# Three 512-column adds through a PSUM tile in place of two adds in SBUF, in a deformable-convolution kernel

## The chip, the cores and the metric

The kernel runs on one core of a Trainium2 chip. Five engines run side by side, each through its own queue in program order: TensorE (PE, with weight loads shown as PEld), VectorE (DVE), ScalarE (ACT), GpSimd (POOL) and SyncE (SP, which here only issues DMAs). The metric is device time in microseconds of one launch; a smaller one is better. Three runs of the kernel before gave 7886.47, 7887.33 and 7905.6 us, median 7887.33 us.

## The reference: what is computed

The input is x, 2 images of 128 channels and 64 x 64 pixels, f32. Two "metaformer" layers follow each other, each with a token mixer and a feed-forward part, both with normalization ahead and a residual sum. The change lies in the mixer of layer 0: four branches of deformable convolution with kernels of 1, 1, 3 and 7 pixels, 60 taps in all. For each pixel and tap, a predicted offset gives a position between pixels; the input is sampled there bilinearly, scaled by a predicted mask, and multiplied with the tap's weights:

```python
return v00 * (1 - wy) * (1 - wx) + v01 * (1 - wy) * wx + v10 * wy * (1 - wx) + v11 * wy * wx
...
sampled = bilinear_sample(x, py, px) * mask[:, None]
return jnp.einsum('bckhw,ock->bohw', sampled, reg_w.reshape(O, C, k * k))
```

The other parts are: group norm, ReLU and a 1 x 1 "fuse" convolution behind the branches; a mixture of 8 experts (layer 0, feed-forward); a convolution and a state-space scan (layer 1, mixer); and 64 experts that pick their tokens (layer 1, feed-forward).

## The kernel before, in words

**Tiling.** An image is 4096 pixels, 32 tiles of 128. Four tiles (512 pixels) are a group (`GT = 4`), so that an image has 8 groups (`NG`). `L0Conv.run` calls `sample(b, g, ...)` for the 8 groups of image 0 and then for those of image 1. A call goes through the 60 taps, so there are 2 x 8 x 60 = 960 taps in all.

**A tap.** A table in DRAM holds, for each pixel position, the 128 channels of its four neighbours (the corners) side by side, 512 numbers. `gather` (L705) has POOL issue four indirect DMAs, one for each tile: 128 rows of the table, chosen by the index list `idx`, go into `v`, a tile of 128 partitions x 4 tiles x 512 numbers in SBUF. Six buffers of `v` exist (pool `l0v`), and a buffer is taken again once PE has transposed what it held. Then:

- L746: DVE multiplies all 2048 columns of `v` with the four corner weights, which it reads from `pw`, a PSUM tile that L738 fills once for 30 taps. The weight is repeated over the 128 channels.
- L748 and L749: DVE adds the corners, first two and two (1024 columns), then the two sums (512 columns), all in `v`.
- L111: PE transposes the four 128 x 128 sums into the PSUM tile `pst`; L753: ACT copies it to `st`.
- L773 (`product`, two taps later): PE multiplies `st` with the tap's weights `regw` and accumulates the branch in two PSUM tiles `out`. At a branch's end, ACT copies them out (L787).

**The order of the work around it.** Everything is written out by hand, in one program order for each engine. The gather of tap t+1 is written ahead of the multiply of tap t; POOL has nothing else to do meanwhile and runs ahead as far as free buffers of `v` let it. After each tap `conv.step()` adds a piece of the offset convolution of a later group (matmuls on PE at L402, sums at L499 and small arithmetic at L545 to L581 on DVE, which make the indices and the corner weights), and `rest.step()`, called `pace` times, adds a piece of other work: during image 0 the normalization of image 1 and constants, during image 1 what follows image 0's sampling (`after`: the fuse convolution, the layer-0 experts with DVE work at L985 and L1001, and the layer-1 convolutions, whose matmuls are L1146, L1154 and L1173). So this other work is paced by taps. The state-space scan and the last feed-forward part come after the sampling of image 1.

**PSUM.** During the sampling, `p_w` has one bank, `p_t` two, `p_o` two, and the offset convolution or the other work two.

Of the kernel before, what the change touches and what calls it, by code (L numbers as in the profile page):

```python
# [10 lines left out]
F32 = mybir.dt.float32  # L11
I32 = mybir.dt.int32
AF = mybir.ActivationFunctionType
ALU = mybir.AluOpType
AX = mybir.AxisListType
PSUM = bass.MemoryType.PSUM
# [3 lines left out]
P = 128  # L20
B = 2
C = 128
# [3 lines left out]
GT = 4  # L26
# [138 lines left out]
def mixed(gens, n):  # L165

    todo, live = deque(gens), deque()
    while todo or live:
        if todo and len(live) < n:
            live.append(todo.popleft())  # L170
        gen = live.popleft()
        try:
            weight = next(gen)
            live.append(gen)
            yield weight
        except StopIteration:
            pass


def together(gens, n):  # L180
    for _ in mixed(gens, n):
        pass


class L0Conv:
# [416 lines left out]
    def run(self, build, after):  # L602

        env, tc, nc = self.env, self.env.tc, self.env.nc
        pools = lambda ctx: lambda name, bufs, **kw: ctx.enter_context(tc.tile_pool(name=name, bufs=bufs, **kw))
        with ExitStack() as ctx:
            pool = pools(ctx)
            self.rp, self.regw = pool("l0rw", 1), {}
            self.ip = pool("l0i", 2)
            self.vp = pool("l0v", 6)  # L610
            self.stp = pool("l0s", 2)
            self.pending, self.held = [], deque()
            first = ctx.enter_context(ExitStack())
            self.open_offsets(pools(first))
            for i in range(2):
                nc.vector.memset(self.padc[i], 0.0)
            psum = ctx.enter_context(ExitStack())
            right = lambda name: pools(psum)(name, 1, space=PSUM, side="right")
            self.p_f = deque([right("l0po")])
            cur = self.new_group(self.ip)  # L620
            with (
                tc.tile_pool(name="nrm", bufs=3) as sp,
                tc.tile_pool(name="nrmp", bufs=4, space=PSUM) as pp,
            ):
                xs = []
                for g in range(NG):
                    if g % GT == 0:
                        x = self.vp.tile([P, GT, 4 * C], F32, name="v")
                    xs.append(x[:, g % GT, :])
                    nc.sync.dma_start(out=xs[g], in_=env.d["x"][0, :, g * 512 : (g + 1) * 512])  # L630
                xn = self.vp.tile([P, GT, 4 * C], F32, name="v")
                self.load_weights()
                for _ in self.zero_table(0):
                    pass
                own = lambda g: xn[:, g % GT, :].rearrange("p (j c) -> p j c", c=C)
                norms = [self.norm_group(0, g, sp, pp, "nrm", x, own(g)) for g, x in enumerate(xs)]
                together(norms[:2], 2)

                stage = self.rows(0, 0)
                self.sum_weights()  # L640
                others = Side()
                others.add(mixed(norms[2:], 3))
                for _ in range(24):
                    others.step()
                offsets = self.offset_stream([(0, 0, cur)], stage)
                while others.todo:
                    next(offsets)
                    for _ in range(3):
                        others.step()
                self.load_chunk(0)  # L650
                for _ in self.norm_end(0):
                    pass
                for _ in offsets:
                    pass
            self.p_w = pool("l0pw", 1, space=PSUM)
            self.p_t = pool("l0pt", 2, space=PSUM)
            self.p_o = pool("l0py", 2, space=PSUM)
            self.pending = [(n, functools.partial(self.load_chunk, c)) for n, c in ((1, 1), (3, 2))]
            early = psum.enter_context(ExitStack())
            p_m = pools(early)("l0pm", 1, space=PSUM, side="right")  # L660

            def more():

                early.close()
                self.p_f.append(right("l0po2"))
                yield


            conv, rest = Side(), Side()
            self.late, self.made = deque(), [0, 0]  # L670
            rest.add(self.norm(1, p_m, "misc"), more(), build)
            ahead = {}

            def runs():
                for g in range(1, NG):
                    ahead[g] = self.new_group(self.ip)
                    yield 0, g, ahead[g]
                    yield 1, g - 1, None
                yield 1, NG - 1, None

            conv.add(self.offset_stream(runs()))
            for g in range(NG):
                self.sample(0, g, *cur, conv, rest, 2 if g else 3, lambda: ahead.get(g + 1))
                cur = ahead.get(g + 1)
            conv.drain()
            rest.drain()
            psum.close()
            first.close()
            side = ctx.enter_context(tc.tile_pool(name="l0ps", bufs=2, space=PSUM))
            rest.add(after(0, side))  # L690
            cur = self.load_group(1, 0)
            for g in range(NG):
                nxt = self.load_group(1, g + 1) if g + 1 < NG else None
                self.sample(1, g, *cur, conv, rest, 2, lambda: nxt)
                cur = nxt
            for f in self.late:
                f()
            for _, f in self.pending:
                f()
            self.pending = []  # L700
            rest.drain()
# [10 lines left out]
    def sample(self, b, g, idx, w4, conv, rest, pace, after):  # L712

        env, nc = self.env, self.env.nc
        pw, vs = None, {}
        new = lambda: self.vp.tile([P, GT, 4 * C], F32, name="v")

        def fetch(idx, t):
            if t in vs:
                v = vs.pop(t)  # L720
                self.gather(b, v, idx, t, range(2, GT))
            else:
                v = new()
                self.gather(b, v, idx, t, range(GT))
            return v

        if b == 0 and g == 0:
            for i in range(6):
                vs[i] = new()
                self.gather(b, vs[i], idx, i, range(0, 2))  # L730
        if not self.held:
            self.held.append(fetch(idx, 0))
        for br, (k, _) in enumerate(BRANCH):
            for t in range(FIRST[br], FIRST[br] + k * k):
                tw = t % HT
                if tw == 0:
                    pw = self.p_w.tile([P, GT, HT, 4], F32, name="pw")
                    nc.vector.tensor_copy(pw, w4[:, :, t : t + HT, :])  # L738
                if t + 1 < NTAP:
                    self.held.append(fetch(idx, t + 1))  # L740
                elif after():
                    self.held.append(fetch(after()[0], 0))
                v = self.held.popleft()
                v4 = v.rearrange("p j (q c) -> p j q c", q=4)
                w = pw[:, :, tw, :].unsqueeze(3).to_broadcast([P, GT, 4, C])
                nc.vector.tensor_tensor(v4, v4, w, ALU.mult)  # L746
                up = v4[:, :, 0:2, :]
                nc.vector.tensor_tensor(up, up, v4[:, :, 2:4, :], ALU.add)  # L748
                nc.vector.tensor_tensor(v4[:, :, 0, :], v4[:, :, 0, :], v4[:, :, 1, :], ALU.add)  # L749
                pt = self.p_t.tile([P, GT, P], F32, name="pst")  # L750
                transpose4(nc, env.ident, pt, [v4[:, j, 0, :] for j in range(GT)])
                st = self.stp.tile([P, 512], F32, name="st", bufs=3)
                nc.scalar.copy(st, pt.rearrange("p j t -> p (j t)"))  # L753
                self.late.append(functools.partial(self.product, b, g, br, t, st))
                if len(self.late) > 2:
                    self.late.popleft()()
                due = [f for n, f in self.pending if n == 0]
                self.pending = [(n - 1, f) for n, f in self.pending if n]
                for f in due:
                    f()  # L760
                conv.step()
                for _ in range(pace):
                    rest.step()
# [1135 lines left out]
```

## Time and profile before

| | us |
|---|---|
| median of the runs | 7887.33 |
| profiled execution, own time | 7901.31 |
| its span | 7898.7 |
| first and last gather start (L705) | 106.8 and 5734.0 |
| DVE busy | 6077.1 |
| PE busy | 5390.6 |
| POOL busy | 5031.9 |
| mean granted TensorE clock | 0.806 of full speed |

How to read it: all times are from one profiled execution. Some 5630 of the 7900 us are the sampling of the two images, the part in which L705, L746, L748 and L749 run. The 40-slice rows of the page show a busy DVE and POOL and DMA engines between 6 and 8 tenths busy there:

```profile
DVE  5878878888887887788898667787756665789992
...
POOL 4777777777777777777777666676743334357640
PEclk8888788888788878878878778877886788877789
DMA  7887767777676778877777777777754344434444
```

In a group's row, "idle before" is the time in which the engine did nothing just ahead of these instructions, and the arrow names what ended most of it. DVE instructions that follow each other without a wait overlap by some 0.08 us in the records.

### The profile page before, as it was taken

What the parts mean: (1) busy time and instruction counts of PE and PEld (TensorE: products, weight loads), DVE (VectorE), ACT (ScalarE), POOL (GpSimd) and SP (SyncE); (2) the same over time, 40 slices, a digit from 0 to 9 for tenths busy, and PEclk for the clock granted to TensorE, in tenths of its full rate; (3) what the DMA queues carried; (4) which work ended last, traced back from release to release, by engine and by line L of the source; (5) the groups of instructions that cost most, each with busy time, mean ns of one, the idle gap of its engine ahead of it and who ended that gap; (6) DMA issues with size and microseconds to landing.
All of it is one profiled execution on the core that took longest, in us unless ns stands there. A gap on an engine that the chain in (4) does not pass through costs nothing. (4 is left out here: it accounts for less than half of the span.)

```text
span 7898.7 us, 67414 instructions
## 1 busy us (share of the span) xinstructions
PE 5390.6 (68%) x21313; PEld 3209.2 (41%) x21313; DVE 6077.1 (77%) x6780; ACT 1992.0 (25%) x3838; POOL 5031.9 (64%) x4589
## 2 busy tenths in 40 slices
PE   4667777667776757656666878865565679756668
PEld 3344444444444424324334555532233456412124
DVE  5878878888887887788898667787756665789992
ACT  1211111111111113211111222211163255455540
POOL 4777777777777777777777666676743334357640
PEclk8888788888788878878878778877886788877789
DMA  7887767777676778877777777777754344434444
GB/s 223 261 267 214 224 207 223 214 219 219 210 221 208 224 228 270 265 255 234 240 237 217 217 218 218 228 224 222 206 172 141 107 114 113 114 131 146 146 137 149
DMA packets 645198, 1596.67 MB, mean 202 GB/s; under 512 B 168020, under 2 KB 253180, under 8 KB 640876
## 3 DMA queue, kind: packets, MB, share of 16 engines
q0 software_dynamic: 307200, 1006.88, 42.5%
q1 hardware_dynamic: 306156, 537.52, 21.4%
q10 hardware_dynamic: 31488, 47.97, 1.7%
q8 instruction: 171, 2.80, 0.1%
q14 instruction: 183, 1.50, 0.1%
HBM read 1478.65 MB, written 115.83 MB: 202 GB/s over the span
## 5 line engine op out<-in xcount | busy, mean ns | idle before, releaser
L705 POOL DMA_INDIRECT v<-table,idx x3840 | 4070.0, 1060 | 1628.2 <-issue 1033.8
L746 DVE TENSOR_TENSOR v<-v,pw 128x2048 f32<-128x2048 f32 x960 | 2192.0, 2283 | 665.7 <-DMA v<-table,idx 466.9
L773 PE MATMUL out<-st,regw 128*128 128x512 f32 x3840 | 2270.7, 719 | 187.6 <-issue 118.6
L753 ACT COPY st<-pst 128x512 f32<-128x512 f32 x960 | 557.7, 585 | 4227.9 <-remote 1887.3
L111 PE MATMUL pst<-ident,v 128*128 128x128 f32 x3840 | 730.7, 318 | 1133.6 <-issue 962.4
L748 DVE TENSOR_TENSOR v<-v 128x1024 f32<-128x1024 f32 x960 | 1177.2, 1226 | 34.6 <-remote 1.6
L1420 POOL TENSOR_TENSOR db<-du,bcb 128x512 f32<-128x512 f32 x512 | 656.8, 1288 | 845.3 <-DVE da L1471 698.8
L773 PEld LDWEIGHTS out<-st,regw 128*128 128x128 f32 x3840 | 807.2, 233 | 864.6 <-issue 779.9
L111 PEld LDWEIGHTS pst<-ident,v 128*128 128x128 f32 x3840 | 522.4, 164 | 1512.3 <-issue 1284.6
L1443 PE MATMUL py<-sc,ident 128*128 128x512 f32 x1024 | 660.7, 752 | 230.7 <-DVE sc L1481 230.3
L1471 DVE TENSOR_TENSOR_SCAN da<-da,state,db 128x512 f32<-128x512 f32 x512 | 657.1, 1283 | 183.2 <-ACT da L1427 137.6
L749 DVE TENSOR_TENSOR v<-v 128x512 f32<-128x512 f32 x960 | 664.4, 692 | 33.0
L402 PE MATMUL po<-wa,win 128*128 128x147 f32 x2112 | 381.7, 303 | 118.1 <-issue 110.8
L402 PEld LDWEIGHTS po<-wa,win 128*128 128x128 f32 x2112 | 334.3, 201 | 228.7 <-issue 228.6
L1443 PEld LDWEIGHTS py<-sc,ident 128*128 128x128 f32 x1024 | 200.4, 229 | 529.9 <-DVE sc L1481 438.0
L1146 PEld LDWEIGHTS ps<-ipw,hs 128*120 128x120 f32 x2816 | 356.0, 207 | 121.7 <-ACT X L1108 56.4
L1146 PE MATMUL ps<-ipw,hs 128*120 128x64 f32 x2816 | 355.1, 290 | 55.2 <-ACT X L1108 40.5
L1481 DVE TENSOR_TENSOR sc<-da,bcb 128x512 f32<-128x512 f32 x512 | 354.2, 692 | 43.0 <-PE py L1443 0.5
L1427 ACT ACTIVATE da<-delta,w_A_log 128x512 f32<-128x512 f32 x512 | 354.0, 692 | 18.7 <-DVE delta L1383 2.8
L1154 PE MATMUL ps<-tm,X 120*88 120x48 f32 x2048 | 216.1, 280 | 52.1 <-ACT Y L1108 35.5
L1154 PEld LDWEIGHTS ps<-tm,X 120*88 120x88 f32 x2048 | 211.0, 187 | 98.7 <-ACT Y L1108 47.4
L402 PEld LDWEIGHTS po<-wb,win 128*128 128x128 f32 x960 | 164.2, 210 | 117.2 <-issue 117.1
(296 smaller groups left out, 4704.3 us busy)
## 6 DMA issues: line engine op xcount, KB each, us to landing
bcb<-bc SPq DMA_DIRECT2D x256, 512.0 KB
regw<-in_regw SPq DMA_DIRECT2D x192, 640.0 KB
v<-table,idx POOLq DMA_INDIRECT x3840
yd<-ys ACTq DMA_DIRECT2D x128, 256.0 KB
yc<-yd SPq DMA_DIRECT2D x32, 1024.0 KB
gb<-gd SPq DMA_DIRECT2D x16, 2048.0 KB
wt<-in_weight SPq DMA_DIRECT2D x32, 1024.0 KB
tm<-pos SPq DMA_DIRECT2D x16, 1440.0 KB
```

Source lines behind the costliest of these rows:

```text
L111: nc.tensor.transpose(ps[:, j, :], s, ident)
L402: m()
L705: self.env.nc.gpsimd.indirect_dma_start(out=v[:, j, :], out_offset=None, in_=self.table[b], in_offset=bass.IndirectOffsetOnAxis(ap=idx[:, ...
L746: nc.vector.tensor_tensor(v4, v4, w, ALU.mult)
L748: nc.vector.tensor_tensor(up, up, v4[:, :, 2:4, :], ALU.add)
L749: nc.vector.tensor_tensor(v4[:, :, 0, :], v4[:, :, 0, :], v4[:, :, 1, :], ALU.add)
L753: nc.scalar.copy(st, pt.rearrange("p j t -> p (j t)"))
L773: nc.tensor.matmul(self.out[half], self.regw[t // CH][:, t % CH, half * P : (half + 1) * P], st, start=first, stop=last,)
L1146: nc.tensor.matmul(ps[:, k, :], patch, own, start=True, stop=True)
L1420: nc.gpsimd.tensor_tensor(dbs[u], pieces[k]["du"][:, half, :], bcb[u // 2][:, 0, :], ALU.mult)
L1443: nc.tensor.matmul(py[k, half], by, what, start=first, stop=last)
L1471: nc.vector.tensor_tensor_scan(s, s, dbs.pop(u), state[:, half, n : n + 1], ALU.mult, ALU.add)
```

## The change

A tap's three DVE operations become four. The multiply is the same operation on the same columns. Then corners 0 and 1 are added into `low`, a tile of 512 columns in PSUM; corner 2 is added to `low` in place; and `low` plus corner 3 goes to the place in `v` from which PE transposes. The order of the sum changes from (0+2)+(1+3) to ((0+1)+2)+3. `low` comes from a new PSUM pool `p_r` with one buffer. The gathers, the transposes and all instructions of the other engines stay, in the same order. In the changed kernel the multiply is L747, the adds are L749, L750 and L751, and other lines after them move down by two.

```diff
@@ -653,6 +653,7 @@
             self.p_w = pool("l0pw", 1, space=PSUM)
+            self.p_r = pool("l0pr", 1, space=PSUM)
             self.p_t = pool("l0pt", 2, space=PSUM)
@@ -742,11 +743,12 @@
                 v4 = v.rearrange("p j (q c) -> p j q c", q=4)
-                w = pw[:, :, tw, :].unsqueeze(3).to_broadcast([P, GT, 4, C])
-                nc.vector.tensor_tensor(v4, v4, w, ALU.mult)
-                up = v4[:, :, 0:2, :]
-                nc.vector.tensor_tensor(up, up, v4[:, :, 2:4, :], ALU.add)
-                nc.vector.tensor_tensor(v4[:, :, 0, :], v4[:, :, 0, :], v4[:, :, 1, :], ALU.add)
+                w = pw[:, :, tw, 0:4].unsqueeze(3).to_broadcast([P, GT, 4, C])
+                nc.vector.tensor_tensor(v4[:, :, 0:4, :], v4[:, :, 0:4, :], w, ALU.mult)
+                low = self.p_r.tile([P, GT, C], F32, name="low")
+                nc.vector.tensor_tensor(low, v4[:, :, 0, :], v4[:, :, 1, :], ALU.add)
+                nc.vector.tensor_tensor(low, low, v4[:, :, 2, :], ALU.add)
+                nc.vector.tensor_tensor(v4[:, :, 0, :], low, v4[:, :, 3, :], ALU.add)
                 pt = self.p_t.tile([P, GT, P], F32, name="pst")
```

## The prediction

> **What bounds the kernel now.** First the page: busy shares and the groups by cost.
>
> ```profile
> PE 5390.6 (68%) x21313; PEld 3209.2 (41%) x21313; DVE 6077.1 (77%) x6780; ACT 1992.0 (25%) x3838; POOL 5031.9 (64%) x4589
> ...
> L705 POOL DMA_INDIRECT v<-table,idx x3840 | 4070.0, 1060 | 1628.2 <-issue 1033.8
> L746 DVE TENSOR_TENSOR v<-v,pw 128x2048 f32<-128x2048 f32 x960 | 2192.0, 2283 | 665.7 <-DMA v<-table,idx 466.9
> ...
> L748 DVE TENSOR_TENSOR v<-v 128x1024 f32<-128x1024 f32 x960 | 1177.2, 1226 | 34.6 <-remote 1.6
> ...
> L749 DVE TENSOR_TENSOR v<-v 128x512 f32<-128x512 f32 x960 | 664.4, 692 | 33.0
> ```
>
> By busy share VectorE (DVE) looks like the bound, and the change gives it more work. But it sits waiting for gathers at L746, so POOL, which issues them, comes next. The line view of L705 and the POOL timeline show how POOL spends a tap:
>
> ```profile
> L705 POOL DMA_INDIRECT v<-table,idx x3840: 940/946/1999, 106.8 to 5734.0; - x192
> ```
> ```profile
> 1240.26 0.94 POOL L705 DMA_INDIRECT v<-table,idx  x1 [0.30 <-issue]
> ...
> 1245.70 0.95 POOL L705 DMA_INDIRECT v<-table,idx  x1 [0.30 <-issue]
> 1246.95 1.83 POOL L705 DMA_INDIRECT v<-table,idx  x1 [0.30 <-issue]
> 1249.08 0.95 POOL L705 DMA_INDIRECT v<-table,idx  x1 [0.30 <-issue]
> ```
>
> The same time on DVE:
>
> ```profile
> 1244.42 2.28 DVE L746 TENSOR_TENSOR v<-v,pw 128x2048 f32<-128x2048 f32 x1
> 1246.73 1.22 DVE L748 TENSOR_TENSOR v<-v 128x1024 f32<-128x1024 f32 x1
> 1247.99 0.69 DVE L749 TENSOR_TENSOR v<-v 128x512 f32<-128x512 f32 x1
> ```
>
> An undisturbed gather takes 0.946 us and is followed by a fixed 0.30 us. So the "64%" misleads: over the sampling stretch (106.8 to 5735 us, 5628 us) POOL needs 3840 x 0.946 = 3633 us busy, 3840 x 0.30 = 1152 us between gathers, and 437 us (4070 less 3633) that some gathers take beyond 0.946. That is 5222 us, 93%; its other waits are the rest.
>
> The 437 us is the key. The gather at 1246.95 started 0.22 us into an L748 and took 1.83 us. Going through all rows of the two timelines: gathers that start 0.04 to 1.1 us into an L748 end 0.82 us after that L748 does, so they lose its remaining time less 0.125 us; all such gathers together lose 420 us. The 700 with over 0.2 us left lose 0.592 us each. Those that start inside an L749 lose by the same formula (6 of them, 0.287 us). Of 1490 that start inside an L746, which is longer but whose second operand pw lies in PSUM, none is held: mean loss 0.001 us. Five that start inside L499's `to<-po,obias` (first operand PSUM, second SBUF): 0.000. So two SBUF operands hold a gather; one PSUM operand does not.
>
> Who leads whom: counting gathers started when an L746 starts, POOL is about one tap ahead in most of the stretch, but about 3 (of at most 5) at 250-500 and 3500-4250 us. The windows and DVE's waits show the three kinds of stretch:
>
> ```profile
> 1000.00:1250.00 250.00, 180.66 (x705) 112.88 (x703) 205.38 (x220) 39.18 (x74) 183.30 (x175) 0.82 0.71 215
> 3750.00:4000.00 250.00, 163.08 (x588) 91.20 (x587) 219.54 (x263) 41.04 (x72) 188.58 (x171) 0.81 0.75 238
> 4500.00:4750.00 250.00, 199.95 (x1063) 143.79 (x1064) 167.01 (x125) 54.62 (x119) 169.12 (x160) 0.78 0.80 223
> ```
>
> Columns: PE, PEld, DVE, ACT, POOL busy, granted clock, DMA share, GB/s. The first (A: 750-3500, 5250-5740; 563 taps) is paced by POOL. The second (B: 250-750, 3500-4250; 215 taps) by DVE, which there hardly waits for a gather. In the third (C: 4250-5250; 162 taps) PE, at a clock of 0.78, has the layer-1 convolutions too; DVE waits for gathers, and POOL for buffers that PE's transposes free.
>
> **The change, part by part.** The multiply keeps operands and shape: 2283 ns, no change. All other engines keep their instruction order; DVE gets 960 rows more.
>
> *Removed on DVE:* L748 and L749. From the start of L748 to the next L746 in back-to-back taps: 1.26 + 0.61 us.
>
> *Added:* three 512-column adds. Prices: with a PSUM source L1001 (512 columns) takes 687 ns and L1523 686; into PSUM, L738's copy of 480 columns takes 653 ns, as long as its columns need at the slope of L748 and L749 (1.04 ns each, 500 ns) plus the 153 ns these also have. So 0.69 us each. The pause between dependent operations is 0.035 us (after L746 and L748); a dependence through PSUM appears only from L738 to L746, at 0.09 us. The chain becomes 2 x (0.69 + pause) + 0.61 us, which is 2.06 us with 0.035 and 2.17 with 0.09, against 1.87: plus 0.19 or 0.30 us a tap. I take 0.19, because the new adds, like L748 and L749, each wait for one instruction of their own queue, while L746 waits for four DMAs as well. Over 960 taps: 182 us (bound 288). What stands behind it on DVE is the next multiply and the offset arithmetic; who waits for DVE is PE's transposes and through them POOL's buffers.
>
> *Freed on POOL:* only the first add still has two SBUF operands, 0.69 us instead of 1.92. If gathers start at the same phases, those up to 0.57 us into the first add (335 in the rows) still lose their remainder less 0.125, 101 us in all. The loss falls from 420 to 101, about 0.33 us a tap, 319 us. Bounds: if every tap held one gather, by 0.26 us on average, 250 us would stay; if nothing were freed, the whole 420.
>
> *The sum* cannot be 319 us: DVE, which is busy all but 1005 of the 5610 us of sampling (pauses over 0.15 us), would need 4605 + 182 = 4787 us, POOL 5222 - 319 = 4903 us. Two engines that used to be 13% apart become equal, with at most six buffers between them. So by stretch, giving each piece the smaller gain of two: three quarters (319 of 420) of POOL's loss in it, or DVE's waits at L746 less 0.19 us a tap.
> - A: POOL's loss 246 us, 184 saved; DVE has 321 us of such waits against 107 us of new work, but not at the same places. In pieces of 250 us the smaller gains add up to 136 us, in pieces of 60 us to 89. Middle: -112.
> - B: DVE has 22 us of waits against 41 of new work: +20.
> - C: POOL's share is 50 us; buffers return through PE, whose work per tap is unchanged, so I credit a little over half: -28.
>
> Together -120 us. With 0.30 us a tap, in the same way: A -78, B +43, C -25, together -60. Were DVE never in the way: -184 - 50, -234. The L0 start and everything after 5740 us stay. PSUM gains a one-buffer tile used by DVE alone, so no other engine waits for it. Before's profiled execution is 7901.31 us (span 7898.7), 14 above the median; so 7781 in its terms, 7767 in the median's.
>
> [...]
>
> **Rivals.**
> - *POOL's full gain* (chance 0.15): DVE's waits move to where they are needed. For: 582 us of waits at L746 in all. Against: B, and buffers that PE returns late. -184 to -240, about 7670.
> - *The bounds swap and nothing is left* (0.10): 0.30 us a tap and gains only where both have slack, A -53, B +48, C -15: 7867, and up to 24 us either side of no change (0.3% of 7887, about what a measurement can tell).
> - *Nothing freed on POOL* (0.08): the second and third add hold gathers too, since they read and write v. Against: L746 and `to<-po,obias`. DVE's 0.19 us is then paid in B (+41) and half in A (+53): 7980.
> - *Adding in place in PSUM is slow* (0.08; slower): the second add reads and writes the same PSUM tile, which no row shows. At one element each two cycles it would take 0.53 us more, 0.72 us a tap. A: 405 less 321 of waits; B: 155 less 22; C covered: +217 if every wait were usable, with half of A's and B's 343 us usable +390, so between 8104 and 8277, about 8190. It decides from about 0.55 us a tap, where A's new work (310 us) uses up its waits.
> - Slower by something else, a PE that lags more among it: 0.04.
>
> **How the numbers follow.** The forecast, -30 to -184, has 0.55, with its own range 7700 to 7857. Faster 0.55 + 0.15 and a little of the swap: 0.71; same 0.09; slower 0.20. The range starts at the full gain (7640) and ends at 7920, where the clearly slower cases begin; that leaves out some 0.05 below and 0.15 above.
>
> **What the changed profile would show.** L705's mean falls from 1060 to about 977 ns (319 us over 3840), and its long gathers end at 1.5 us instead of 2.0. The three adds read near 690 ns with pauses of 0.035 us. POOL's waits for PE and "remote" grow; L746's for DMA shrink in A. 3500-4250 gets longer by some 10 us. The forecast is wrong if the second add is well over 0.7 us, if gathers starting inside the second or third add are still held, or if PE's lag takes up the gain.

## The result, and the profile after

The changed kernel takes 7912.95 us (median of 9 runs, 7894.91 to 7922.09) against 7888.05 us for the kernel before (9 runs): ratio 1.0024, 95% interval 1.0013 to 1.0036. That is 25 us more, at the edge of what a measurement of this kernel tells from no change. Forecast was 120 us less.

The cost table of the changed kernel's page:

```profile
L706 POOL DMA_INDIRECT v<-table,idx x3840 | 3747.4, 976 | 1954.1 <-issue 1002.8
L747 DVE TENSOR_TENSOR v<-v,pw 128x2048 f32<-128x2048 f32 x960 | 2190.3, 2282 | 476.7 <-DMA v<-table,idx 323.0
...
L749 DVE TENSOR_TENSOR low<-v 128x512 f32<-128x512 f32 x960 | 673.6, 702 | 36.1 <-remote 2.3
L750 DVE TENSOR_TENSOR low<-low,v 128x512 f32<-128x512 f32 x960 | 671.2, 699 | 33.0
L751 DVE TENSOR_TENSOR v<-low,v 128x512 f32<-128x512 f32 x960 | 663.4, 691 | 32.9
```

Every price in it is close to what was forecast. POOL's gathers take 976 ns on average (977 was expected) and lost only 114 us beyond 0.946 us each, instead of 437. The three adds take 702, 699 and 691 ns (690 expected), with pauses of 0.034 to 0.038 us on average (0.035 expected). VectorE (DVE) has about 165 us more of adds, and one more pause in each tap.

So the change did what it was meant to do, and the sampling is still as long as before: from the first to the last multiply 5612 us instead of 5610. The freed 323 us of POOL went into waits. The waits of the gathers, before:

```profile
POOL v L705 <- issue: 1033.8, 3389, 0.6
...
POOL v L705 <- remote: 248.1, 120, 4.8
...
POOL v L705 <- PE pst L111: 123.6, 96, 5.6
```

and after (us in total, number, longest):

```profile
POOL v L706 <- issue: 1002.8, 3262, 2.1
...
POOL v L706 <- remote: 381.6, 148, 6.5
...
POOL v L706 <- PE pst L111: 277.1, 171, 8.0
```

The first row is mostly the fixed 0.30 us between gathers. The other two are gathers for which no buffer of `v` was free, since TensorE (PE) had not yet transposed what the buffer held ("remote" has no releaser in the records, but every one of these waits ended on a semaphore, a counter in the records, which 6540 matmuls of TensorE raise and no other engine's instructions do). In waits of over 0.32 us ahead of gathers, what POOL waited beyond the fixed 0.30 us was 459 us before and is 785 us now: plus 326, where the gathers gave 323 back. Some 70 us of such a sum lie ahead of the first gather, in every run. Of the plus 326, 284 us stand in waits that ended on TensorE's semaphore (337 us before, 621 now). Group by group it is the same: in groups 1 to 8 of the 16, counted from 0 (60 taps each, 342 to 353 us), the gathers lost 22 to 31 us per group and now lose 5 to 8, while POOL's other waits went from 17 to 23 us to 35 to 45.

How TensorE falls behind shows in its timeline, here at one place. The changed kernel, TensorE from 2084 us:

```profile
2084.21 1.55 PE L402 MATMUL po<-wc,win 128*128 128x180 f32 x4 [5.27 <-ACT win L455]
2085.57 0.40 PE L111 MATMUL pst<-ident,v 128*128 128x128 f32 x1
2086.97 0.37 PE L111 MATMUL pst<-ident,v 128*128 128x128 f32 x1 [1.00 <-issue]
2088.39 0.37 PE L111 MATMUL pst<-ident,v 128*128 128x128 f32 x1 [1.05 <-issue]
2089.80 0.37 PE L111 MATMUL pst<-ident,v 128*128 128x128 f32 x1 [1.03 <-issue]
2091.20 3.41 PE L775 MATMUL out<-st,regw 128*128 128x512 f32 x4 [1.03 <-issue]
```

and POOL in the same microseconds:

```profile
2087.80 0.94 POOL L706 DMA_INDIRECT v<-table,idx  x1 [0.30 <-issue]
2091.68 0.97 POOL L706 DMA_INDIRECT v<-table,idx  x1 [2.93 <-PE pst L111]
```

The four transposes of a tap start 1.4 us apart, although nothing in the records holds them. The weight loads of the third and the fourth, at 2087.68 and 2089.10 us, lie halfway, so that each instruction comes 0.70 us after the one before; the four need over 4 us. POOL waits 2.93 us for the buffer that they free. Counting weight loads and matmuls of the sampling that start 0.69 to 0.725 us after their predecessor gives 380 in the kernel before and 393 in the changed one. I call these the 0.70 us steps. They come in bursts of up to some 14 us, mostly in the first 3000 us, where the offset convolution runs. They turned out to separate the sessions in which the kernel before takes 7890 to 7950 us from those in which it takes 7570 to 7600 (the experiments below).

How late TensorE is can be read tap by tap, as the time from the end of a tap's last add to the start of its first transpose. In groups 1 to 8 its median is 5.2 us in the kernel before and 6.8 us in the changed one; in a later session without the steps (e6_before and e5_after) it is 0.10 us in both. The steps that stand in the records may not be all of it: the two traces of record hold 5146 and 5229 counts of TensorE's semaphore, which its matmuls raise 6540 times (6536 and 6531 counts in e6_before and e5_after), so TensorE's records are incomplete there.

### The profile page after: what moved, and what is told of

The parts are those of the page before. It is cut to its first block, busy times and chain, and to the rows that moved or that the text cites. A ratio compares the mean times of both kernels' runs of the same rounds, so it can differ in the third digit from the quotient of the medians.

```text
span 7911.1 us, 68374 instructions
## 1 busy us (share of the span) xinstructions
PE 5345.4 (68%) x21313; PEld 3194.9 (40%) x21313; DVE 6227.1 (79%) x7740; ACT 1988.6 (25%) x3838; POOL 4711.2 (60%) x4589
## 5 line engine op out<-in xcount | busy, mean ns | idle before, releaser
L706 POOL DMA_INDIRECT v<-table,idx x3840 | 3747.4, 976 | 1954.1 <-issue 1002.8
L747 DVE TENSOR_TENSOR v<-v,pw 128x2048 f32<-128x2048 f32 x960 | 2190.3, 2282 | 476.7 <-DMA v<-table,idx 323.0
L749 DVE TENSOR_TENSOR low<-v 128x512 f32<-128x512 f32 x960 | 673.6, 702 | 36.1 <-remote 2.3
L750 DVE TENSOR_TENSOR low<-low,v 128x512 f32<-128x512 f32 x960 | 671.2, 699 | 33.0
L751 DVE TENSOR_TENSOR v<-low,v 128x512 f32<-128x512 f32 x960 | 663.4, 691 | 32.9
```

Source lines behind the costliest of these rows:

```text
L706: self.env.nc.gpsimd.indirect_dma_start(out=v[:, j, :], out_offset=None, in_=self.table[b], in_offset=bass.IndirectOffsetOnAxis(ap=idx[:, ...
L747: nc.vector.tensor_tensor(v4[:, :, 0:4, :], v4[:, :, 0:4, :], w, ALU.mult)
L749: nc.vector.tensor_tensor(low, v4[:, :, 0, :], v4[:, :, 1, :], ALU.add)
L750: nc.vector.tensor_tensor(low, low, v4[:, :, 2, :], ALU.add)
L751: nc.vector.tensor_tensor(v4[:, :, 0, :], low, v4[:, :, 3, :], ALU.add)
```

## The experiments

Each group of runs is a session of its own on one chip, with its own runs of the kernel before. The times of the sessions differ by 5%, so everything below is a ratio to the kernel before of the same session. The runs of record are the two kernels of the section above.

### First session: three adds in SBUF, one add less, one buffer less, release by VectorE

Kernel before: 7593.05 us (7 runs).

**e1_sbuf3**, against the changed kernel:

```diff
-            self.p_r = pool("l0pr", 1, space=PSUM)
...
-                low = self.p_r.tile([P, GT, C], F32, name="low")
+                low = v4[:, :, 0, :]
```

> The changed kernel's three adds, all in SBUF (the partial sum stays in v), so that all three have two SBUF operands and hold POOL's gathers again, some 2.07 us a tap, while VectorE's work is that of the changed kernel. Theory F (the freed POOL time is worth nothing, because POOL spends it waiting for a buffer): within 0.3% of the changed kernel's 7913 us. Theory G (the freed time was worth something and VectorE's longer chain ate it): 100 to 320 us slower than the changed kernel, 8010 to 8230 us, with some 420 us of long gathers on POOL.

Measured: 7544.64 us, ratio 0.9936 (0.992 to 0.9953).

**e2_no_add2**:

```diff
                 nc.vector.tensor_tensor(low, v4[:, :, 0, :], v4[:, :, 1, :], ALU.add)
-                nc.vector.tensor_tensor(low, low, v4[:, :, 2, :], ALU.add)
                 nc.vector.tensor_tensor(v4[:, :, 0, :], low, v4[:, :, 3, :], ALU.add)
```

> The changed kernel without its second add: corner 2 is left out of the sum, so VectorE's chain is 0.73 us a tap shorter (704 us over 960 taps), and all else stays. Theory D (VectorE's own time sets the pace of the sampling): 300 to 500 us faster than the changed kernel, 7400 to 7600 us. Theory B (buffers of v that come back late through TensorE set the pace): 0 to 100 us faster, 7810 to 7913 us, with VectorE's waits for gathers grown by 500 us or more.

Measured: 7282.83 us, ratio 0.9585 (0.9568 to 0.9602).

**e3_v5**:

```diff
-            self.vp = pool("l0v", 6)
+            self.vp = pool("l0v", 5)
...
-            for i in range(6):
+            for i in range(5):
                 vs[i] = new()
```

> The changed kernel with five buffers of v in place of six (the first group fetches five taps ahead). Theory B (late buffers set the pace): the loop through a buffer has one sixth less room, 200 to 600 us slower, 8110 to 8510 us, with POOL's waits grown accordingly. Theory D (VectorE's own time): under 60 us slower, up to 7970 us.

Measured: 7349.15 us, ratio 0.9682 (0.9666 to 0.9698).

**e4_release**, with the edit of e3_v5 and:

```diff
+            self.sup = pool("l0u", 4)
...
-                nc.vector.tensor_tensor(v4[:, :, 0, :], low, v4[:, :, 3, :], ALU.add)
+                su = self.sup.tile([P, GT, C], F32, name="su")
+                nc.vector.tensor_tensor(su, low, v4[:, :, 3, :], ALU.add)
...
-                transpose4(nc, env.ident, pt, [v4[:, j, 0, :] for j in range(GT)])
+                transpose4(nc, env.ident, pt, [su[:, j, :] for j in range(GT)])
```

> The changed kernel with the last add writing to a tile of its own (four buffers of 512 columns) that TensorE transposes from, and five buffers of v: same memory, but a buffer of v is free once VectorE's last add has read it, without TensorE. Theory B: POOL's waits for TensorE vanish and the freed gather time counts, 150 to 320 us faster than the changed kernel, 7590 to 7760 us. Theory D: within 24 us of 7913 us, with VectorE at over 93% of the sampling as before.

Measured: 7362.48 us, ratio 0.9706 (0.9686 to 0.9726).

These expectations were all written in microseconds beside 7913, and the session upset them: the kernel before itself was 295 us faster, and the changed kernel even with a buffer less was 3.2% faster than that. Theory B failed here: a buffer less cost nothing like 200 us, and freeing `v` without TensorE brought nothing. It was not tested for the runs of record by this, since the profiles of the four show a difference: 14 to 23 steps of 0.70 us in the sampling, where the runs of record had 380 and 393.

### Second session: the two kernels themselves, and the buffers of the kernel before

Kernel before: 7573.98 us (25 runs).

**e5_after** and **e6_before** are the two kernels unchanged; **e7_before_v5** has the edit of e3_v5 on the kernel before; **e8_before_release** has, on top of that:

```diff
+                su = self.sup.tile([P, GT, C], F32, name="su")
-                nc.vector.tensor_tensor(v4[:, :, 0, :], v4[:, :, 0, :], v4[:, :, 1, :], ALU.add)
+                nc.vector.tensor_tensor(su, v4[:, :, 0, :], v4[:, :, 1, :], ALU.add)
```

> The changed kernel unchanged, beside the kernel before on this chip, with a profile. In the two runs of record TensorE issued some 370 instructions of the sampling 0.70 us apart one after another (and 130 to 180 at 1.4 us); in the four runs of the first experiments this was 13 to 22, and the kernel before took 7593 us instead of 7888. Theory S (these steps of TensorE make buffers late and hid the gain): where they are absent, the changed kernel is 180 to 280 us faster than before, ratio 0.963 to 0.977, with VectorE idle under 350 us in the sampling; where they are present, ratio 1.00. Theory B6 (six buffers in themselves are worse than five): ratio about 1.00 in either case.

> The kernel before unchanged, for its profile on this chip. Theory S: if it takes about 7590 us, fewer than 50 of TensorE's instructions in the sampling stand 0.70 us apart, POOL's long gathers still lose about 430 us, and POOL's other waits are under 200 us. If it takes about 7890 us, the 370 are back and POOL's other waits are over 400 us.

> The kernel before with five buffers of v. Theory S: POOL paces this kernel through the held gathers, so the sixth buffer matters little, within 40 us of the kernel before. Theory B6 (fewer gathers in flight help by themselves): 150 us or more faster than the kernel before.

> The kernel before with its last add writing to a tile of its own (four buffers) and five buffers of v, so that VectorE frees v without TensorE. Theory S without the steps: POOL is bound by held gathers and not by buffers, within 60 us of the kernel before. With the steps: 100 to 250 us faster than before, since late transposes no longer hold buffers.

Measured: e5_after 7306.66 us, ratio 0.9658 (0.9632 to 0.9684); e6_before 7571.73, with 31 steps, 470 us lost by held gathers and 115 us of other waits (71 of them ahead of the first gather), as theory S expected; e7_before_v5 7596.93, ratio 1.0032 (1.0015 to 1.005); e8_before_release 7584.61, ratio 1.0018 (1.0 to 1.0035).

Here the same change is worth 267 us. The profile of e5_after, gathers and multiply, then the windows (PE, PEld, DVE, ACT, POOL busy, granted clock, DMA share, GB/s):

```profile
L706 POOL DMA_INDIRECT v<-table,idx x3840 | 3720.1, 969 | 1398.9 <-issue 925.4
L747 DVE TENSOR_TENSOR v<-v,pw 128x2048 f32<-128x2048 f32 x960 | 2188.7, 2280 | 183.0 <-DMA v<-table,idx 147.8
```
```profile
1000.00:1250.00 250.00, 182.31 (x823) 119.08 (x821) 240.76 (x298) 48.29 (x87) 189.99 (x198) 0.94 0.79 246
3750.00:4000.00 250.00, 183.14 (x878) 114.70 (x878) 229.16 (x285) 55.23 (x119) 176.31 (x186) 0.85 0.82 249
4500.00:4750.00 250.00, 188.01 (x913) 115.39 (x911) 225.48 (x212) 54.28 (x116) 181.25 (x189) 0.84 0.82 251
```

The same windows in the changed kernel's run of record:

```profile
1000.00:1250.00 250.00, 182.97 (x742) 118.46 (x741) 210.54 (x262) 39.88 (x76) 169.16 (x176) 0.84 0.71 218
3750.00:4000.00 250.00, 164.00 (x612) 92.12 (x611) 220.80 (x298) 40.61 (x71) 166.95 (x171) 0.82 0.74 236
4500.00:4750.00 250.00, 190.92 (x1063) 134.13 (x1063) 180.59 (x171) 55.20 (x119) 155.81 (x162) 0.81 0.80 225
```

Without the steps DVE is busy 241 of 250 us in the first window (211 of record), POOL starts 198 instructions instead of 176, and the granted clock is 0.94 instead of 0.84. A group of 60 taps takes 301 to 308 us (groups 1 to 7) instead of 342 to 353. In groups 1 to 8 no gather waits for a buffer any more. Over all groups these waits are left (the second row is gathers that waited for an earlier gather's landing):

```profile
POOL v L706 <- PE pst L111: 149.7, 167, 6.8
POOL v L706 <- DMA v<-table,idx: 143.0, 382, 5.3
```

against 277 us ("PE pst") and 382 us ("remote") of record. The account of POOL comes out here too: its gathers lost 470 us in e6_before and 87 in e5_after, so 383 us were freed; its other waits grew by 115 (from 115 to 230 us), and the remaining 268 are the gain. With this base the first session can be read again, by its ratios:

- e1_sbuf3 has VectorE's work of the changed kernel and the held gathers of three SBUF adds. It stands at 0.9936, the changed kernel at 0.9658; the difference, 0.028, is some 210 us of 7593. That is what freeing POOL through PSUM is worth, within the 100 to 320 us of theory G; that VectorE's longer chain eats it, G's other half, did not show. It also stands 0.6% below the kernel before, with more work on VectorE: its gathers lost 370 us, those of e6_before 470. An add of 512 columns holds a gather for an estimated 0.57 us at most (0.69 less 0.125, as in the prediction's formula); L748's 1024 columns held one for up to 1.05 in the kernel before of record.
- e2_no_add2 has 704 us less of VectorE's work and gains 0.7 points (55 us) over 0.9658. Its gathers are close to POOL's floor: 3840 x (0.946 + 0.305) = 4804 us, 151 us lost beyond 0.946 and 51 us of other waits behind the first gather, some 5005 us from the first gather to the last (4986 us from the first multiply to the last). VectorE waits 726 us for gathers there. So the changed kernel, with 5027 us from the first multiply to the last, is within 1% of what POOL allows there; theory D is out.
- e3_v5 and e4_release stand at 0.9682 and 0.9706 and so lose 18 and 36 us against 0.9658: with TensorE in time, six buffers are enough.

e7 and e8 show the other side: the kernel before, limited by held gathers, is 23 and 11 us slower with the buffers rearranged (the interval of the second reaches no change). Theory B6 (fewer gathers in flight help) is out.

### Third session: a TensorE made late, on a day when it is late already

The kernel before took 7951.17 us (13 runs), so the steps were back. The edit, on the kernel before (**e9_late_before**), on the changed kernel (**e10_late_after**) and on e4_release (**e11_late_release**); **e12_after** is the changed kernel unchanged:

```diff
                 pt = self.p_t.tile([P, GT, P], F32, name="pst")
+                if t % 5 == 0:
+                    for _ in range(12):
+                        nc.tensor.matmul(pt.rearrange("p j t -> p (j t)"), env.ident, env.zero, start=True, stop=True)
```

> The kernel before with twelve extra 512-column matmuls on TensorE ahead of the transposes of every fifth tap (their result is overwritten), 5 us at full clock, so that TensorE runs late in bursts on a chip where it does not by itself. Theory S: POOL's waits for buffers rise from some 115 us to 300 to 600, and the kernel becomes 50 to 300 us slower than before, since POOL is at its limit and loses what it waits.

> The changed kernel with the same twelve extra matmuls in every fifth tap. Theory S (a late TensorE hides the gain, through buffers of v that come back late): the gain of the changed kernel shrinks from 3.4% to under 1.5% against the kernel before with the same matmuls, with POOL's waits at 500 us or more. Rival (the gain depends on the chip for another reason, gathers or VectorE's speed): the pair keeps a gain of 2.5 to 3.5%.

> The changed kernel with the extra matmuls, and the last add writing to a tile of its own (four buffers) beside five buffers of v, so that VectorE frees v. Theory S with the buffers as the link: at least 60 us faster than the changed kernel with the extra matmuls. If TensorE's lag acts in another way (VectorE waiting for the offset matmuls at L499, or TensorE simply full): within 30 us of it.

> The changed kernel unchanged, on this chip, as the base of the other three: ratio to the kernel before 0.963 to 0.970 if TensorE's instructions rarely stand 0.70 us apart here (then before is near 7580 us), 0.998 to 1.004 if they often do (then before is near 7890 us).

Measured: e12_after 7962.22 us, ratio 1.001 (0.9995 to 1.0024), with 351 steps in its sampling: no gain, as in the runs of record. e9_late_before 8385.1 (1.055; 1.0527 to 1.0573), 434 us more where 50 to 300 were expected. (The expected 5 us are short: in the trace of before, at a granted clock of 1.00, four 512-column rows of L773 take 1.88 us from 2002.43 us, 0.43 us apart, and its 1920 calls stand there as 3840 rows. Twelve calls of two rows are an estimated 10.3 us, where each extra call gives two rows as well.) e10_late_after 8462.11 (1.0646; 1.0608 to 1.0685), so the pair stands at 1.009. It says little, since the gain was gone here anyway. e11_late_release 8833.27 (1.109; 1.1062 to 1.1118) was 371 us slower than e10 where I expected at least 60 us less. Its waits show why:

```profile
POOL v L707 <- DVE su L753: 1672.4, 385, 27.4
```
```profile
DVE su L753 <- remote: 562.3, 130, 9.9
DVE su L753 <- PE pst L111: 424.2, 80, 16.0
```

`v` no longer waits for TensorE, but the last add does, for one of the four `su`, and with it everything behind on VectorE. My reading, which no further run tests: six shared buffers give TensorE more room than five and four split ones, so this layout made the room toward TensorE smaller. The expectation failed, and as a test of theory S the run decides nothing.

### Fourth session: late and relieved, on a day without the steps

Kernel before: 7582.77 us (12 runs). **e15_late_before** and **e16_late_after** are the pair of the third session again. In **e13_few_before** and **e14_few_after** most products are left out, so the branch sums are incomplete:

```diff
-        for half in range(2):
+        for half in range(2) if first or last else ():
             nc.tensor.matmul(
```

> The kernel before, with only the first and the last tap of each branch multiplied with their weights (the products of the other taps are left out), so that TensorE has 1.7 us less to do in most taps and some 4 of 22 matmuls fewer. Theory S: where TensorE's instructions often stand 0.70 us apart (before near 7890 to 7950 us), POOL's other waits fall from some 460 us towards 150, and the time falls by 150 to 350 us. Where they do not (before near 7580), POOL is the limit: within 60 us of before.

> The changed kernel with the same products left out. Theory S: with TensorE relieved, the changed kernel is 2.5 to 4% faster than the kernel before with the same products left out, on either kind of day, because then only POOL and VectorE count. Rival (the gain is lost to something else that differs between the sessions): where before is near 7900 us the pair stays within 1%.

> The kernel before with twelve extra matmuls in every fifth tap, once more. Only new where TensorE's 0.70 us steps are absent (before near 7580 us): theory S then expects 50 to 300 us over before, with POOL's waits at 300 us or more. Where they are present: the ratio of the earlier run, 1.055 within 1%.

> The changed kernel with the same extra matmuls. Where the 0.70 us steps are absent: theory S expects the gain over the kernel before with the same matmuls to shrink from 3.4% to under 1.5%; a rival by which the session, not a late TensorE, decides the gain expects 2.5 to 3.5% to stay. Where the steps are present: no gain, ratio of the pair 1.00 to 1.015 as in the earlier call.

Measured: e15_late_before 7880.36 us (1.0393; 1.0365 to 1.0421), e16_late_after 7836.19 us (1.0334; 1.0315 to 1.0352). The pair stands at 0.994, where the kernels without the extra matmuls stand at 0.966: a late TensorE takes the gain from 3.4% to 0.6%. The steps are absent (10 and 11), so that it is the lateness and not the session. This lateness is of another kind than that of record, though: with the extra matmuls TensorE's weight loads and matmuls together cover 96% of groups 1 to 8 (71 to 72% in the runs of record), and the first transpose starts 10.7 and 11.5 us after the last add (median). TensorE is nearly full here; in the runs of record, by its rows, it was late without being full. In e16's profile POOL's freed time has gone to the same wait as in the runs of record:

```profile
L706 POOL DMA_INDIRECT v<-table,idx x3840 | 3725.2, 970 | 1894.7 <-issue 934.0
```
```profile
POOL v L706 <- PE pst L111: 610.4, 262, 13.8
```

e15, with the held gathers, has 330.8 us in that row.

e13_few_before took 7611.43 us (1.0039; 1.0025 to 1.0054) and e14_few_after 7367.1 us (0.9705; 0.9684 to 0.9726), 0.968 for the pair: the gain stays with little work on TensorE. Neither kernel got faster by the missing products; TensorE's granted clock fell to 0.675 and 0.688 (0.839 to 0.847 in the kernel before of that session).

**e17_few_before** and **e18_few_after** are this last pair again, in the hope of a session with the steps:

> The kernel before with most products left out, as in the earlier pair, which met a session without the 0.70 us steps (before 7583, ratio 1.004). Where before is near 7900 us this time, theory S expects 150 to 350 us less than before (ratio 0.955 to 0.98). Where it is near 7580 us the run only repeats 1.004.

> The changed kernel with the same products left out (earlier: 0.9705 of before, 0.968 of its pair). Where before is near 7900 us this time, theory S expects the pair to show 2.0 to 4% gain, though the changed kernel itself shows none in such a session; a rival by which such sessions lack the gain for another reason expects the pair within 1%.

The session had none (before 7595.61 us). 7609.1 us (1.0025; 1.0008 to 1.0042) and 7370.87 us (0.9691; 0.9673 to 0.9709), 0.969 for the pair, which repeats the earlier one.

**What is shown and what stays open.** Shown: the change frees POOL (e1 against e5), and this is worth 3.4% where TensorE keeps up; in the runs of record POOL spent what it gained in waits that ended on TensorE's semaphore (plus 284 of 326 us); and a TensorE made late takes most of the gain away through buffers that return late (e15 and e16). Only coincidence over the sessions: that in the runs of record the lateness came from the 0.70 us steps. Both sessions with 351 and more steps had no gain, in the others, with 6 to 31, the changed kernel or the variants of it were faster. A session with steps in which TensorE was relieved was not met, so that this brings the gain back is not shown. What causes the steps is open. In e12 the bursts often start 120 to 150 weight loads and matmuls apart, or a multiple of that, from which I guessed at instructions that arrive in blocks and run out; but the instruction loads (171 packets, 2.80 MB on the page of before, 16 KB each) took no longer with the steps than without (median 962 ns in the kernel before of record, 961 in e6_before), so the guess is not shown. The granted clock differs between the sessions too (0.806 against 0.844 in the kernel before); whether as cause or effect, and whether the profiler has a part in the steps, is not shown.

## Why the prediction was wrong

The measured median lies inside the range, but 120 us less were forecast and 25 us more came, so the range held without the sum being right. By its steps:

- *What holds the gathers* was right: two SBUF operands hold them and one does not. The loss left was put at 437 - 319 = 118 us; it was 114. In the changed kernel's run of record, gathers that start inside L749 (two SBUF sources) with over 0.2 us of it left lose 0.293 us each (313 of them); those that start so inside L750 or L751 (one source in PSUM) lose 0.002 us (776 of them).
- *The adds* were right: 0.69 us and 0.035 us of pause, in place through PSUM too, so the rival of a slow second add fell (699 ns; its 0.53 us more was an estimate, 512 columns at a second 1.04 ns each). A source in PSUM made an add no longer: L749, with two SBUF sources, takes 702 ns, L750 and L751, each with one PSUM source, 699 and 691.
- *B* is not confirmed: groups 9 to 11 became 1060 us instead of 1054 (some 10 us were expected for 3500-4250), 6 us in one execution of each, and without the steps they became shorter, 1012 instead of 1019 (e5_after and e6_before).
- *A and C of the sum failed.* They set POOL's saving against VectorE's waits and took POOL's other waits as they were. In the run of record these waits were 459 us; they grew to 785 and took the whole 323 us. Where -112 and -28 us were forecast, groups 2 to 8, which lie in A, became 2414 us instead of 2421, and groups 12 to 14, most of C, 1103 instead of 1112. In the sum, the buffers that come back late through TensorE are a reason for C alone. Elsewhere the prediction saw them: it expected these waits to grow, and its last sign of being wrong is that PE's lag takes up the gain. But it gave them no us in A, and "a PE that lags more" had 0.04 with all else that might go wrong. The trace of before had the evidence: in groups 1 to 8 the first transpose starts 5.2 us (median) after the last add, and POOL waited 2 to 4 us for a buffer about five times in every 250 us of stretch A while it was only about one tap ahead of VectorE, so that most of the six buffers must have been on TensorE's side. I counted these waits by what they cost POOL then, and did not ask what they would be once POOL came earlier.
- The outcome is the rival "the bounds swap and nothing is left" in size (25 us from no change, at the edge of its 24), but not in mechanism: VectorE's longer chain is not what ate the gain. In the second session it has the same chain and the kernel is 267 us faster.
- In that session the sum was too small as well: 267 us against 120, and against 234 for "DVE never in the way". There the gathers gave back 383 us instead of the 319 of the sum, POOL's other waits began at 115 us instead of 459 and took 115 of the 383, and VectorE has 242 us of pauses left in the changed kernel's sampling of 5027 us (685 in e6_before): most of its waits were usable. My pieces of 60 us were too strict a limit where TensorE is in time; that the six buffers level such pieces out is my reading, not shown.

## What to carry to other kernels

When an engine is freed, ask who hands it its next buffer: its other waits can grow by all that it gains (here by 326 us for 323), as long as the slower neighbour does not keep up. A busy share did not show this here (TensorE was busy for 68% of the span before and after); short waits for a buffer did, 2 to 4 us about five times in every 250 us of stretch A, where POOL was only about one tap ahead of VectorE. And a kernel that alternates between two times from session to session has to be compared inside one session: the same change was worth 3.4% in one (e5_after, 0.9658) and nothing in another (e12_after, 1.001).

## What the runs showed that was not expected

- TensorE can issue instructions 0.70 us apart in bursts, in some sessions and not in others: 380 such steps in the sampling against 31 for the same program, and 7888 us against 7574. The second and the third session carried the same chip number; whether it was the same chip, the runs do not tell.
- A gather that starts while VectorE runs an operation with two SBUF operands waits for its end (ahead of the change, 700 gathers with over 0.2 us of an L748 left lost 0.592 us each; with one operand in PSUM, 1490 inside an L746 lost 0.001); splitting 1024 columns into two adds of 512 shortens the loss from 470 to 370 us although VectorE holds the operands longer in total (e6_before and e1_sbuf3).
- An add in place in PSUM runs at the pace of one in SBUF: 699 ns for 512 columns (L750), beside 692 (L749 of the kernel before).
